# Norms of layer 2 beside the 7x7 attention of the next sample, images loaded ahead of the spectra, first transforms interleaved

## The chip, the core and the metric

The kernel runs on one core of a Trainium2 chip, in one launch. All data are float32. The time is the device time of one execution in microseconds (us); lower is better. A core has five engines with an instruction queue each: PE (matrix products, whose weight loads are listed as PEld), DVE and ACT (element-wise work), POOL (GpSimd) and SP, which here issues DMA transfers only. An engine executes its queue in order; between engines, semaphores order the work.

## The reference

Four layers are applied to an image batch `x` of shape (4, 56, 56, 128), each as `x = x + layer(groupnorm(x))`. Layer 0 is an attention over 7x7 windows followed by attention over all 3136 tokens and an MLP; layer 1 is an edge layer; layer 2 is a spectral attention; layer 3 a convolution. The change lies where layer 2 begins:

```python
xa = x.reshape(B * T, 1, H, W)                 # B=4 samples, T=128 channels, 56x56
xa_n = _inorm(xa, norm_g[0], norm_b[0])        # instance norm of each image
k = _fno_layer(xa_n, wK, wKs, bKs, (H // 2, W // 2))
q = _fno_layer(xa_n, wQ, wQs, bQs, (H // 2, W // 2))
v = _fno_layer(xa_n, wV, wVs, bVs, (H, W))
...
xf = jnp.fft.rfft2(x, norm='forward')          # inside _fno_layer, by _spec_conv
...
attention = _inorm(projd + xa, norm_g[1], norm_b[1])
```

Here `x` is already group-normed, in 32 groups of 4 channels, over the whole image. The kernel computes both norms of a sample from the same row statistics and does the Fourier transforms as matrix products.

## The kernel before

Channels lie on the 128 partitions, the 56x56 image of a sample (3136 values, 12.5 KB) along each partition.

**Samples one after the other.** `build` (from L2320 on) runs `first_layers` for b = 0 to 3. It loads `xw` (L2397, SP), calls `fast_attention`, which first calls `fast_windows` (attention in 7x7 windows) and then does the attention over all tokens, then `mlp` and `edge_layer`. These write the result in place into the one tile `x1`, and SP stores it to `x2d[b]` in DRAM (L2403). All of this stands in a branch that is taken when the scores are small; the other branch holds a general form that does not run on these inputs.

**The windows.** `fast_windows` handles the image in NG = 8 groups of 392 tokens (8 windows of 49). It is a software pipeline written out by hand: in iteration n of 19, group n is projected (`project`, L360 to L365), group n-1 scored (L379), n-2 multiplied with the values (`value`, L394 to L398), n-3 transposed (`turn`, L406), n-4 projected out (`output`, L416), and n-5 to n-11 go through a layer norm (`central` L421, `variance` L431 to L436, `divide` L443) and the projections of the next attention (`attended`, L451 to L462). In `variance`, every fourth group (HALF = 4), a root on ACT and a reciprocal on DVE are made for four groups at once (`w_r`, L434 and L435). Three PSUM banks, handed out in turn by `bank()`, take most products. PE, ACT and DVE run in the order in which the code stands (`manual_schedule`); only POOL and SP are left to the scheduler.

**The spectra.** After the fourth sample, `spectra` is the first stage of layer 2. For each sample, `normed_images` takes row statistics (56 `bn_stats` of 56 values, L1188), aggregates them (L1192), averages over the four channels of a group by products with small matrices (`s_pt`, L1194 and L1210), norms the image in place (`apply_norm`, L192, called at L1215), stores it to `xad` for later (L1216), and finds mean and deviation of each row of the instance norm (L1219 to L1233, two more `s_pt` products) into `st.norm`. `sample_spectra` then transforms along rows (112 pairs of products into `s_pr`, L1250, in four quarters, each scaled into tile `s_z` by DVE at L1252 and copied by ACT at L1254), and from `s_z` makes three sets of spectra: `s_ps` (L1260, copied to S and iS by ACT at L1263), `s_pr2` (L1272, listed as `s_pr`, copied to R at L1276) and `s_px` (32 products in eight banks, L1282, copied to `xh` by DVE and ACT in turn, L231 and L229). The fourth sample comes first, since its image is still in `x1`; the other three are loaded again from `x2d` into two tiles (L1182). Both functions are generators: the norm of the next sample is advanced by one step after each step of the present sample's spectra. `value_weights` and `all_score_weights` prepare weights on POOL at the same time. `attention_weights` follows the stage; it uses S, iS and R.

Of the kernel before, what the change touches and what calls it, by code (L numbers as in the profile page):

```python
# [11 lines left out]
F32 = mybir.dt.float32  # L12
# [6 lines left out]
P = 128  # L19
B = 4  # L20
HH = 56
# [277 lines left out]

def both_attentions(k, w, xw, xf):  # L300
    window_attention(k, w, xw, xf)
    global_attention(k, w, xf)


def fast_windows(k, w, xw, xf, mr, Q, K, V):

# [15 lines left out]
    with ExitStack() as es:  # L322
# [103 lines left out]
        def variance(g):  # L426
            q = g % HALF
            if q == 0:
                roots[g // HALF] = psum.tile([P, 512], F32, tag="var", name="w_var", bufs=1)
            var = roots[g // HALF]  # L430
            nc.tensor.matmul(var[32 * q:32 * q + 32, :N], k.ones_c[:, 0:32], squares.pop(g), start=True, stop=True)  # L431
            if q == HALF - 1:
                r = wk.tile([P, N], F32, name="w_r")
                nc.scalar.activation(r, var[:, :N], AF.Sqrt, scale=1024.0, bias=eps)  # L434
                nc.vector.reciprocal(r, r)  # L435
                roots[g // HALF] = r  # L436
# [9 lines left out]
        def attended(g):  # L446
# [7 lines left out]
            while chunk < 25 and (g == NG - 1 or chunk * P + 4 * P <= b.stop):  # L454
# [8 lines left out]
                chunk += m  # L463

        norm(0)
        norm(1)
        for n in range(NG + 11):
            for stage, g in ((norm, n + 2), (project, n), (score, n - 1), (value, n - 2), (turn, n - 3), (output, n - 4),
                             (central, n - 5), (variance, n - 6), (attended, n - 11), (divide, n - 10)):
                if 0 <= g < NG:  # L470
                    stage(g)


# [85 lines left out]

def fast_attention(k, w, xw, xf, mr):  # L560

# [8 lines left out]
    with ExitStack() as es:  # L570
# [3 lines left out]
        va = big.tile([P, 25, P], F32, name="f_va")  # L574
        fast_windows(k, w, xw, xf, mr, qT, kT, va)

# [589 lines left out]

def normed_images(k, w, st, b, pools, x2d, xad, ready):

    nc = k.nc
    wk, psum = pools

    def tiny(name):
        return wk.tile([P, HH], F32, name="s_" + name)

    if st.last == b:
        xp = st.x1
    else:
        xp = wk.tile([P, HH + 1, HH], F32, name="s_x2")  # L1180
        for t in range(0, HH, 28):
            nc.sync.dma_start(xp[:, t:t + 28, :], x2d[b, :, t:t + 28, :])  # L1182
        yield
    nc.vector.memset(xp[:, HH, :], 0.0)
    x = xp[:, :HH, :]
    rows = wk.tile([P, HH, 6], F32, name="s_rows")
    for t in range(HH):
        nc.vector.bn_stats(rows[:, t, :], x[:, t, :])  # L1188
        if t % 8 == 7:
            yield  # L1190
    mv = wk.tile([P, 2], F32, name="s_mv")
    nc.vector.bn_aggr(mv, rows.rearrange("p a b -> p (a b)"))  # L1192
    ps = psum.tile([P, 512], F32, tag="t", name="s_pt")
    nc.tensor.matmul(ps[:, 0:1], k.g4, mv[:, 0:1], start=True, stop=True)  # L1194

    half = [rows[:, :, i] for i in range(6)]
    mean, sq, d = tiny("mean"), tiny("sq"), tiny("d")
    nc.vector.tensor_sub(d, half[1], half[4])
    nc.vector.tensor_mul(d, d, d)
    nc.vector.tensor_add(sq, half[2], half[5])  # L1200
    nc.vector.scalar_tensor_tensor(sq, d, HH / 4, sq, ALU.mult, ALU.add)
    nc.vector.tensor_add(mean, half[1], half[4])
    yield
    mr = wk.tile([P, 2], F32, name="s_mr")
    t1 = wk.tile([P, 1], F32, name="s_t1")
    nc.vector.tensor_copy(mr[:, 0:1], ps[:, 0:1])
    nc.vector.tensor_sub(t1, mv[:, 0:1], mr[:, 0:1])
    nc.vector.tensor_mul(t1, t1, t1)
    nc.vector.tensor_add(t1, t1, mv[:, 1:2])
    nc.tensor.matmul(ps[:, 1:2], k.g4, t1, start=True, stop=True)  # L1210
    yield
    nc.scalar.activation(t1, ps[:, 1:2], AF.Sqrt, bias=k.eps)
    yield
    nc.vector.reciprocal(mr[:, 1:2], t1)
    apply_norm(k, x, x, mr)  # L1215
    nc.sync.dma_start(xad[b], x)  # L1216
    ready[b] = xp
    yield
    nc.vector.tensor_scalar(mean, mean, 0.5, mr[:, 0:1], ALU.mult, ALU.subtract)  # L1219
    nc.vector.tensor_scalar_mul(mean, mean, mr[:, 1:2])  # L1220
    nc.vector.tensor_scalar(sq, sq, mr[:, 1:2], mr[:, 1:2], ALU.mult, ALU.mult)
    nc.tensor.matmul(ps[:, 64:64 + HH], k.ones_c, mean, start=True, stop=True)
    yield
    nc.vector.tensor_copy(st.norm[:, b, 0, :], ps[:, 64:64 + HH])
    nc.vector.tensor_sub(d, mean, st.norm[:, b, 0, :])
    nc.vector.tensor_mul(d, d, d)
    nc.vector.scalar_tensor_tensor(sq, d, float(HH), sq, ALU.mult, ALU.add)
    nc.tensor.matmul(ps[:, 128:128 + HH], k.ones_px, sq, start=True, stop=True)
    yield
    nc.scalar.activation(d, ps[:, 128:128 + HH], AF.Sqrt, bias=k.eps)  # L1230
    yield
    nc.vector.reciprocal(d, d)
    nc.vector.tensor_scalar_mul(st.norm[:, b, 1, :], d, w.ng[:, 0:1])  # L1233
    yield


def sample_spectra(k, st, b, pools, x):

# [4 lines left out]

    z = wk.tile([P, 33, 2 * HH], F32, name="s_z")
    xf = x.rearrange("p t h -> p (t h)")
    for t0 in range(0, HH, 14):
        ps = psum.tile([P, 512], F32, tag="row", name="s_pr")
        for t in range(14):
            for ri in range(2):
                nc.tensor.matmul(ps[64 * ri:64 * ri + 64, t * 33:(t + 1) * 33],  # L1250
                                 xf[:, (t0 + t) * HH:(t0 + t) * HH + 64], k.fw[:, ri, :], start=True, stop=True)
        nc.vector.tensor_mul(z[:, :, t0:t0 + 14], ps[:, :462].rearrange("p (t f) -> p f t", t=14),  # L1252
                             bc(st.norm[:, b, 1, t0:t0 + 14], 1, 33))
        nc.scalar.copy(z[:, :, HH + t0:HH + t0 + 14], z[:, :, t0:t0 + 14])  # L1254
        yield
    o = slice(64 * (b % 2), 64 * (b % 2) + 64)
    for c0, c1, v in C_BLOCKS_S:
        ps = psum.tile([P, 512], F32, tag="acc", name="s_ps")
        m = (c1 - c0) * HH
# [8 lines left out]
    for blocks in (C_BLOCKS_R[:2], C_BLOCKS_R[2:]):  # L1268
        ps = psum.tile([P, 512], F32, tag="acc", name="s_pr2")
        for i, (c0, c1, v) in enumerate(blocks):  # L1270
# [8 lines left out]
    for c0 in range(0, 32, 4):  # L1279
        ps = psum.tile([P, 512], F32, tag="acc", name="s_px")  # L1280
        for i in range(4):
# [5 lines left out]

def spectra(k, w, st, x2d, xad):

# [3 lines left out]
    for t in (st.S, st.iS, st.R):  # L1293
        nc.gpsimd.memset(t[:, :, :, HH:], 0.0)
    ready = {}
    with ExitStack() as es:
# [4 lines left out]
                                                     mybir.EngineType.DVE}))  # L1301

        order = [st.last] + [b for b in range(B) if b != st.last]
        norms = [normed_images(k, w, st, b, (wk, tiny), x2d, xad, ready) for b in order] + [iter(())]
        next(norms[1])
        for _ in norms[0]:
            pass
        for n, b in enumerate(order):
            ahead = norms[n + 1]
            for _ in sample_spectra(k, st, b, (wk, psum), ready.pop(b)):  # L1310
                next(ahead, None)
            for _ in ahead:
                pass

# [1032 lines left out]
def build(k, packs, I, out):  # L2347
# [3 lines left out]
    with ExitStack() as es:  # L2351
# [10 lines left out]

        l2p = es.enter_context(tc.tile_pool(name="l2", bufs=1))
        with tc.tile_pool(name="w01", bufs=1) as wp, tc.tile_pool(name="io", bufs=1) as io:
            xw = io.tile([P, TOK], F32, name="xw")
# [29 lines left out]
            def first_layers(attention, x, to, loaded=False):  # L2395
# [6 lines left out]
                edge_layer(k, w1, x1, st)  # L2402
                nc.sync.dma_start(to, x1)  # L2403

            with tc.If(small_scores > 0) as small:
                for b in range(B):
                    first_layers(lambda *a: fast_attention(*a, k.mr[:, b, :]), I["x"][b], x2d[b],
                                 loaded=b == 0)
            with small.Else():
                with tc.For_i(0, B, 1) as b:  # L2410
                    first_layers(both_attentions, I["x"][bass.ds(b, 1)].rearrange("b p t -> (b p) t"),
                                 x2d[bass.ds(b, 1)].rearrange("b p l n -> (b p) l n"))

        l3p = es.enter_context(tc.tile_pool(name="l3", bufs=1))
        load_weights(k, l3p, I, "w3_", w2)
        load_weights(k, l3p, I, "w2_", w2, only=CONV_WEIGHTS)
        st = Env()
        st.x1, st.last = x1w, B - 1
        st.norm = l3p.tile([P, B, 2, HH], F32, name="norm")
        st.AbT = l3p.tile([P, 2, HH], F32, name="AbT")  # L2420
        st.dc = l3p.tile([1, B, HH], F32, name="dc")
        with tc.tile_pool(name="xh", bufs=1) as xp:
            st.xh = xp.tile([112, B, 2, 32, HH], F32, name="xh")
            with tc.tile_pool(name="sp", bufs=1) as sp:
# [4 lines left out]
                with tc.tile_pool(name="g_wk", bufs=1, side="right") as wk:  # L2429
                    all_score_weights(k, I, w2, sp, wk, st)  # L2430
                    value_weights(k, I, w2, wk, dd)
                    spectra(k, w2, st, x2d, xad)
                x1s.close()
# [32 lines left out]
```

## Time and profile before

| | |
|---|---|
| median of 5 runs | 3930.84 us (3921.26 to 3940.58) |
| the profiled execution | 3928.13 us, span 3926.3 us |
| mean granted PE clock | 0.955 |
| busy PE / DVE / ACT / POOL | 3551.4 / 2883.7 / 2050.1 / 1200.9 us (90 / 73 / 52 / 31%) |
| DMA | 111.12 MB, mean 28 GB/s |
| x2d stores of samples 0 to 3 issued | first at 762.2, last at 2896.6 us |
| spectra stage | from the last edge operation (DVE, 2895.83 + 0.68) to the last copy of xh (ACT, 3037.73 + 0.53) |

The profile gives, for each instruction, its line, engine, operation, output and inputs, its start and length, and how long its engine had been idle before it and on whom it had waited ("[3.47 <-DVE s_mv L1192]"). "Granted clock" is the share of the full PE clock that the chip allowed. The chain of waits is followed back from the last instruction to whatever released each one. A tile is shown without its number, so `s_x2` appears as `s_x`, `w_h1` as `w_h` and `x1` as `x`.

### The profile page before, as it was taken

The numbers are of one execution on the slowest core, as the hardware profiler recorded it, in microseconds if no ns is written. First come the engines' busy times: TensorE is split into PE (matmuls) and PEld (weight loads), VectorE is DVE, ScalarE is ACT, GpSimd is POOL, SyncE is SP. The second block draws the span as 40 slices with busy tenths as digits, with TensorE's granted clock in tenths as the row PEclk, the third lists the DMA queues.
The fourth block names the chain that finished last, engine by engine and source line by source line (L and its number), as shares of the span: only waits on it lengthen the run. The fifth ranks groups of instructions, "written<-read, shape, count | busy, mean of one in ns | idle before, by whom it ended". The sixth has DMA issues, their size and how long they took to land. (4 is left out here: it accounts for less than half of the span.)

```text
span 3926.3 us, 79380 instructions
## 1 busy us (share of the span) xinstructions
PE 3551.4 (90%) x35416; PEld 1589.5 (40%) x35416; DVE 2883.7 (73%) x2667; ACT 2050.1 (52%) x2056; POOL 1200.9 (31%) x671
## 2 busy tenths in 40 slices
PE   6899998989998899999889999998977989999988
PEld 4322234542223455222245532224446433336554
DVE  6588867758887685888768568885975767775764
ACT  4577755557775444777555467773532002215332
POOL 0000006600000560000037100001860769984665
PEclk9999999999999999999999999998978999999988
DMA  2000000000000000000000000000022048842101
GB/s 94 1 1 1 1 1 19 19 1 1 1 1 1 18 3 18 1 1 1 1 17 3 18 1 1 1 1 0 3 77 96 1 91 165 176 95 83 58 9 50
DMA packets 73496, 111.12 MB, mean 28 GB/s; under 512 B 62140, under 2 KB 63932, under 8 KB 67900
## 3 DMA queue, kind: packets, MB, share of 16 engines
q1 hardware_dynamic: 14460, 93.13, 8.0%
q10 hardware_dynamic: 58688, 12.85, 2.0%
q8 instruction: 279, 4.57, 0.5%
q14 instruction: 69, 0.57, 0.0%
HBM read 79.46 MB, written 26.51 MB: 27 GB/s over the span
## 5 line engine op out<-in xcount | busy, mean ns | idle before, releaser
L641 ACT ACTIVATE f_ring<-f_s 128x1792 f32<-128x1792 f32 (+3 forms) x796 | 1098.5, 1430 | 316.6 <-PE f_s L639 314.4
L594 DVE TENSOR_TENSOR f_acc<-f_acc,f_ring 128x1792 f32<-128x1792 f32 x560 | 1134.0, 2025 | 81.1 <-ACT f_ring L641 27.2
L639 PE MATMUL f_s<-f_qT,f_kT 32*128 32x448 f32 x5376 | 740.5, 573 | 57.9 <-ACT f_ring L641 33.7
L883 POOL TENSOR_TENSOR x<-xf,xw 128x343 f32<-128x343 f32 (+2 forms) x36 | 29.9, 832 | 2129.6 <-issue 2057.3
L600 PE MATMUL f_po<-f_ring,f_va 128*32 128x448 f32 x5376 | 592.0, 548 | 0.0
L967 DVE TENSOR_TENSOR e_td<-e_pa,e_c 128x1792 f32<-128x1792 f32 x252 | 491.4, 2014 | 8.0 <-ACT e_a L934 8.0
L969 POOL TENSOR_TENSOR e_tp<-e_a,e_c 128x1792 f32<-128x1792 f32 x140 | 451.7, 3259 | 144.5 <-PE e_acc L974 104.6
L639 PEld LDWEIGHTS f_s<-f_qT,f_kT 32*128 32x128 f32 x5376 | 268.5, 183 | 539.0 <-ACT f_ring L641 369.7
L974 PE MATMUL e_acc<-e_td,t_shared 32*32 32x448 f32 x8064 | 322.3, 545 | 23.6 <-DVE e_td L967 13.1
L971 ACT ACTIVATE e_tp<-e_tp 128x1792 f32<-128x1792 f32 x140 | 235.2, 1697 | 184.9 <-POOL e_tp L969 184.9
L1568 DVE TENSOR_TENSOR u_ud<-u_px,u_d 112x1792 f32<-112x1792 f32 x144 | 240.1, 1708 | 95.1 <-PE u_po L1573 86.0
L600 PEld LDWEIGHTS f_po<-f_ring,f_va 128*32 128x32 f32 x5376 | 133.0, 109 | 399.9 <-issue 398.9
L974 PE MATMUL e_acc<-e_tp,t_shared 32*32 32x448 f32 x4480 | 220.6, 544 | 2.5 <-ACT e_tp L971 2.2
L1573 PE MATMUL u_po<-u_ud,AT 112*64 112x448 f32 x960 | 200.7, 548 | 23.7 <-DVE u_ud L1568 23.7
L1570 POOL TENSOR_TENSOR u_up<-xh,u_d 112x1792 f32<-112x1792 f32 x64 | 193.7, 3056 | 24.1 <-PE u_po L1573 12.4
L974 PEld LDWEIGHTS e_acc<-e_td,t_shared 32*32 32x32 f32 x8064 | 133.6, 103 | 149.0 <-DVE e_td L967 59.0
L594 DVE TENSOR_TENSOR f_acc<-f_ring 128x1792 f32<-128x1792 f32 x28 | 56.7, 2024 | 106.5 <-ACT f_ring L641 77.5
L1573 PE MATMUL u_po<-u_up,AT 112*64 112x448 f32 x576 | 125.1, 541 | 0.9 <-POOL u_up L1570 0.9
L1573 PEld LDWEIGHTS u_po<-u_ud,AT 112*64 112x64 f32 x960 | 64.8, 137 | 148.0 <-issue 86.6
L974 PEld LDWEIGHTS e_acc<-e_tp,t_shared 32*32 32x32 f32 x4480 | 94.4, 103 | 54.7 <-ACT e_tp L971 18.5
L856 ACT ACTIVATE m_hT<-m_ph,w_fb 128x392 f32<-128x392 f32 x128 | 72.8, 589 | 73.0 <-PE m_ph L855 67.5
L612 DVE RECIPROCAL f_den<-f_s 128x448 f32<-128x448 f32 x28 | 82.8, 2956 | 37.6 <-PE f_s L610 37.6
(460 smaller groups left out, 4752.8 us busy)
## 6 DMA issues: line engine op xcount, KB each, us to landing
u_d<-dd SPq DMA_DIRECT2D x48, 784.0 KB
xw<-in_x SPq DMA_DIRECT2D x4, 1568.0 KB
x2d<-x SPq DMA_DIRECT2D x4, 1568.0 KB
x_xs<-xad ACTq DMA_DIRECT2D x32, 196.0 KB
xm<-x_ev ACTq DMA_DIRECT2D x64, 98.0 KB
o_a<-xm SPq DMA_DIRECT2D x8, 784.0 KB
o_x<-x2d SPq DMA_DIRECT2D x4, 1568.0 KB
out<-o_o SPq DMA_DIRECT2D x12, 448.0 KB
```

What stands on the lines that cost most here:

```text
L594: nc.vector.tensor_add(acc, slots(j, 0) if c == 1 else acc, slots(j, c))
L600: nc.tensor.matmul(po[heads[h], :NB], va[o, c, heads[h]], p, start=(c == 0), stop=(c == 24))
L612: nc.vector.reciprocal(den, pd[:, 0, :NB])
L639: nc.tensor.matmul(ss[:, i, :NB], kT[heads[h], c * P:(c + 1) * P], qT[heads[h], blk(j)], start=True, stop=True)
L641: nc.scalar.activation(ring[:, slot:slot + m, :], ss[:, :m, :NB], AF.Exp, scale=scale)
L967: nc.vector.tensor_tensor(t, am, cm, ALU.max)
L969: nc.gpsimd.tensor_sub(t, bc(a.rearrange("p (l n) -> p l n", l=8), 1, 4), cm)
L971: nc.scalar.activation(tf, tf, AF.Relu)
L974: nc.tensor.matmul(acc[quarters[q], r, :NB], k.ident[o, o], t[o, q].rearrange("p l n -> p (l n)"), start=(g == 0), stop=(g == len(EDGE_TUR ...
L1568: nc.vector.tensor_mul(u, bc(px[:, :, :NB], 2, m), dm)
L1570: nc.gpsimd.tensor_mul(u, bc(x, 2, m), dm)
L1573: nc.tensor.matmul(po[64 * b2:64 * b2 + 64, :NB], st.AT[:, 8 * i + h0 + q, 2 * bp + b2, :], u[:, b2, q, :], start=(left == 16), stop=(left ...
```

## The change

**The norms move.** `normed_images` is now started by `first_layers` and handed to `fast_windows` as `beside`. While sample b goes through its windows (b = 1, 2, 3), the image of sample b-1, still in `x1`, is normed in place. One step follows each iteration n, except in n = 9 and 13, where the step (a root on ACT) stands inside `variance`, behind the root of `w_r`. The steps: 14 `bn_stats` in each of n = 0 to 3; aggregate, first product, five small operations and a copy in n = 4; three small ones in n = 5; second product and ACT's copy in n = 6; root in n = 9; reciprocal, `apply_norm`, store to `xad` and three small ones in n = 10; third product and four operations in n = 11; fourth product and copy in n = 12; root in n = 13; reciprocal and a scaling in n = 14. The products take banks of the windows' own `bank()`. The roots now read a copy in SBUF instead of PSUM. The norm of sample 3 stays in `spectra`, beside the spectra of samples 0 and 1.

**Images.** The normed images of samples 0, 1 and 2 are loaded from `xad`, not from `x2d`, into two tiles of a new pool `x2` on the right-hand side of SBUF. The loads of 0 and 1 are issued right after the branch, ahead of all weight loads. The store of sample 3 to `x2d` is issued after them. `st.norm` is allocated earlier, and the zero row below an image is written by POOL instead of DVE.

**Transforms.** `sample_spectra` is split. `first_transform` holds the row transform. `spectra` does the transform of sample 0 whole; then, within the spectra of sample b, the four quarters of the transform of b+1 stand after steps 2, 5, 7 and 9 of 13. The order of samples is 0, 1, 2, 3. The pool of PSUM tag "acc" has four banks instead of three.

The branch that does not run gets the same norms in a loop of its own after its samples; it is left out below.

```diff
@@ fast_windows
             if q == HALF - 1:
                 r = wk.tile([P, N], F32, name="w_r")
                 nc.scalar.activation(r, var[:, :N], AF.Sqrt, scale=1024.0, bias=eps)
+                next(steps, None)
                 nc.vector.reciprocal(r, r)
...
+        steps = beside(bank)
         norm(0)
         norm(1)
         for n in range(NG + 11):
...
                 if 0 <= g < NG:
                     stage(g)
+            if n not in (HALF + 5, 2 * HALF + 5):
+                next(steps, None)
+        for _ in steps:
+            pass
@@ normed_images
-def normed_images(k, w, st, b, pools, x2d, xad, ready):
+def normed_images(k, w, st, b, wk, bank, xp, xad):
...
-    if st.last == b:
-        xp = st.x1
-    else:
-        xp = wk.tile([P, HH + 1, HH], F32, name="s_x2")
-        for t in range(0, HH, 28):
-            nc.sync.dma_start(xp[:, t:t + 28, :], x2d[b, :, t:t + 28, :])
-        yield
-    nc.vector.memset(xp[:, HH, :], 0.0)
...
         nc.vector.bn_stats(rows[:, t, :], x[:, t, :])
-        if t % 8 == 7:
+        if t % 14 == 13:
             yield
...
-    ps = psum.tile([P, 512], F32, tag="t", name="s_pt")
+    ps = bank()
     nc.tensor.matmul(ps[:, 0:1], k.g4, mv[:, 0:1], start=True, stop=True)
...
+    nc.vector.tensor_copy(mr[:, 0:1], ps[:, 0:1])
     yield
...
     nc.vector.tensor_add(t1, t1, mv[:, 1:2])
+    yield
+    ps = bank()
     nc.tensor.matmul(ps[:, 1:2], k.g4, t1, start=True, stop=True)
-    yield
-    nc.scalar.activation(t1, ps[:, 1:2], AF.Sqrt, bias=k.eps)
+    var = wk.tile([P, 1], F32, name="s_var", bufs=1)
+    nc.scalar.copy(var, ps[:, 1:2])
+    for _ in range(3):
+        yield
+    nc.scalar.activation(t1, var, AF.Sqrt, bias=k.eps)
     yield
     nc.vector.reciprocal(mr[:, 1:2], t1)
     apply_norm(k, x, x, mr)
-    nc.sync.dma_start(xad[b], x)
-    ready[b] = xp
-    yield
+    nc.sync.dma_start(xad, x)
...
+    yield
+    ps = bank()
     nc.tensor.matmul(ps[:, 64:64 + HH], k.ones_c, mean, start=True, stop=True)
-    yield
...
+    yield
+    ps = bank()
     nc.tensor.matmul(ps[:, 128:128 + HH], k.ones_px, sq, start=True, stop=True)
+    nc.scalar.copy(d, ps[:, 128:128 + HH])
     yield
-    nc.scalar.activation(d, ps[:, 128:128 + HH], AF.Sqrt, bias=k.eps)
+    nc.scalar.activation(d, d, AF.Sqrt, bias=k.eps)
@@ spectra
-        for _ in norms[0]:
+        norm = normed_images(k, w, st, B - 1, wk, lambda: tiny.tile([P, 512], F32, name="s_pt"), st.x1, xad[B - 1])
+        zs = {}
+        first = [first_transform(k, st, b, (wk, psum), st.x1 if b == B - 1 else images(b), zs) for b in range(B)]
+        for _ in first[0]:
             pass
-        for n, b in enumerate(order):
-            ahead = norms[n + 1]
-            for _ in sample_spectra(k, st, b, (wk, psum), ready.pop(b)):
-                next(ahead, None)
-            for _ in ahead:
-                pass
+        for b in range(B):
+            for n, _ in enumerate(sample_spectra(k, st, b, (wk, psum), zs.pop(b))):
+                next(norm, None)
+                if b < B - 1 and n in (2, 5, 7, 9):
+                    next(first[b + 1])
@@ build
-                nc.sync.dma_start(to, x1)
+                if to is not None:
+                    nc.sync.dma_start(to, x1)
+
+            def norms(b, bank):
+                if b < 0:
+                    return iter(())
+                return normed_images(k, w2, st, b, io, bank, x1w, xad[b])
...
                 for b in range(B):
-                    first_layers(lambda *a: fast_attention(*a, k.mr[:, b, :]), I["x"][b], x2d[b],
-                                 loaded=b == 0)
+                    first_layers(lambda *a: fast_attention(*a, functools.partial(norms, b - 1), k.mr[:, b, :]), I["x"][b],
+                                 x2d[b] if b < B - 1 else None, loaded=b == 0)
...
+        x2p = x2s.enter_context(tc.tile_pool(name="x2", bufs=2, side="right"))
+
+        def images(b):
+            if b not in loaded:
+                xp = loaded[b] = x2p.tile([P, HH + 1, HH], F32, name="s_x2")
+                for t in range(0, HH, 28):
+                    nc.sync.dma_start(xp[:, t:t + 28, :], xad[b, :, t:t + 28, :])
+                nc.gpsimd.memset(xp[:, HH, :], 0.0)
+            return loaded[b]
+
+        loaded = {}
+        for b in range(2):
+            images(b)
+        nc.sync.dma_start(x2d[B - 1], x1)
```

## The prediction

> **What bounds the kernel now.** I looked first at the chain of waits between 2880 and 3050 us, because the change empties this stretch, the spectra stage. Its columns are start, length and what ran.
>
> ```profile
> 2898.86 6.71 DVE s_rows L1188 x56
> ...
> 2917.68 12.12 PE s_pr L1250 x224
> ...
> 2998.19 1.68 DVE s_mv L1192
> 2999.91 0.48 PE s_pt L1194 x2
> ...
> 3019.46 7.19 PE s_pr L1250 x224
> 3027.46 1.23 PE s_ps L1260 x4
> ...
> 3031.93 5.77 PE s_px L1282 x56
> ```
>
> The chain hops between DVE (norms) and PE (transforms), so the stage is bound by neither alone. The same stage as a timeline of PE, with the idle time before each group in brackets:
>
> ```profile
> 2999.91 0.48 PE L1194 MATMUL s_pt<-s_mv,t_shared 128*128 128x1 f32 x2 [3.47 <-DVE s_mv L1192]
> ...
> 3010.38 0.65 PE L1222 MATMUL s_pt<-s_mean,c_ones_c 128*128 128x56 f32 x2 [2.49 <-DVE s_mean L1220]
> ...
> 3027.46 1.87 PE L1260 MATMUL s_ps<-s_z,t_images 128*128 128x56 f32 x6 [0.84 <-DVE s_z L1252]
> 3029.26 1.07 PE L1272 MATMUL s_pr<-s_z,t_images 128*64 128x448 f32 x6
> 3030.84 6.85 PE L1282 MATMUL s_px<-t_images,s_z 128*112 128x112 f32 x64 [0.51 <-ACT iS L1263]
> ```
>
> PE stands while DVE makes the next sample's norm, four times a sample. The last sample, with no norm beside it, takes 1.87 + 1.07 + 6.85 us. Third, busy time by stretch (length; PE, PEld, DVE, ACT, POOL busy; granted PE clock; DMA):
>
> ```profile
> 2980.00:2985.00 5.00, 4.47 (x23) 4.47 (x24) 1.11 (x4) 0.74 (x2) 0.00 (x0) 0.50 0.30 125
> ...
> 3020.00:3025.00 5.00, 5.00 (x170) 5.00 (x167) 1.28 (x2) 1.19 (x3) 0.00 (x0) 0.95 0.01 3
> ...
> 761.00:861.00 100.00, 88.83 (x729) 54.94 (x728) 53.88 (x102) 47.74 (x80) 8.77 (x22) 0.97 0.04 17
> 2896.50:3038.30 141.80, 94.95 (x1232) 83.81 (x1232) 82.98 (x362) 34.29 (x77) 36.07 (x57) 0.74 0.32 115
> ```
>
> The stage lasts 141.8 us with a clock of 0.74: the waits also cost clock (0.50 in 2980 to 2985, where the 64 matmul records of s_px go at half pace). The 7x7 windows of sample 1 (761 to 861), where three norms go, have DVE busy 54 of 100 us but PE 89 of 100. So half of DVE is free there, but its gaps are waits inside a chain with PE. The timeline, DVE then PE:
>
> ```profile
> 776.29 0.62 DVE L224 TENSOR_SCALAR w_qd<-w_mm,t_first 32x392 f32<-32x392 f32 x1 [2.14 <-ACT w_qd L222]
> ...
> 782.56 0.21 DVE L397 RECIPROCAL w_rec<-w_po 128x8 f32<-128x8 f32 x1 [0.66 <-PE w_po L394]
> ...
> 829.29 0.57 DVE L424 COPY w_h<-w_mm 128x392 f32<-128x392 f32 x1 [2.92 <-ACT w_sq L423]
> ```
> ```profile
> 820.00 0.82 PE L416 MATMUL w_mm<-w_oT,t_first 128*128 128x392 f32 x2
> ...
> 824.85 0.92 PE L443 MATMUL w_mm<-w_r,c_ones 32*128 32x392 f32 x2 [2.42 <-ACT w_oT L229]
> 825.71 1.65 PE L416 MATMUL w_mm<-w_oT,t_first 128*128 128x392 f32 x2
> ```
>
> From 776 to 824 PE shows no wait; any DVE delay there that reaches PE is lost for good. And after 2.42 us of idling, the same matmul took 1.65 us in place of 0.82.
>
> **The spectra stage, gain.** It ends at 3038.3, with ACT's last copy of xh. In the changed kernel it starts with the first transform of sample 0, whose image is already normed. DVE's last edge operation ends at 2896.5 and its next starts at 2898.9 (2.35 us of issue after the branch); I take 2898.9 for PE too. A transform at full clock took 6.73 us (the one at 2954.14), so 2905.6; 0.84 to s_ps: 2906.4.
> - Sample 0. PE does s_ps 1.87, the first quarter of the next transform 1.7 and s_pr2 1.07, to 2911.1. Then s_pt stands ahead of s_px in PE's order and needs s_mv. DVE by then has 42 statistics (6.71/56 = 0.12 us each, 5.0 us), one s_z 0.64, 14 more (1.7) and the aggregate 1.67: 2915.3. PE idles some 4.2 us. Left for PE: s_px 6.85, three quarters of a transform 5.1, four norm products about 2.0 (0.38, 0.59, 0.40, 0.68), some 14 us; the second product waits another 0.5 for DVE, which also prepares layer-3 weights. For the half clock after the idle I add 3 us (the bounds are 0, and 12 where s_px and transform all go at half pace). 2915.3 + 14 + 0.5 + 3: end 2932.8.
> - Samples 1 and 2: 1.87 + 1.07 + 6.85 + 6.9 = 16.7 us each, no norm beside them except the last two steps. ACT has 8.1 us of copies in each, DVE 5, so PE is the bound. The fourth PSUM bank of "acc" keeps s_px off ACT's copies. End 2966.2.
> - Sample 3: 10.8 us, as from 3027.46 to 3038.3. End 2977.0.
>
> Gain 61.3 us; 69 without the clock and s_mv losses, 50 with a late image (a rival below). POOL's weight preparation started on a load that landed at 2903.9 and handed its last result to SP at 2944.9; it still starts on a load behind the same last edge sample, ends before 2977, and what then follows on every engine is unchanged.
>
> **The queues.** SP's loads of images 0 and 1 come after the branch. Their tile lies where 25 KB of attention tiles lay, by the sizes in the code clear of the edge layer's tiles, so they can land around 2600, hidden under 300 us of edge layer. Sample 3's x2d store and the weight loads stand behind them and still go at about 2897. Image 2's load stands behind twelve weight loads (SP issued them by 2908 before) and is needed at about 2935. x2d plus weights plus image, 5.6 MB by my count of the sizes, at the 292 GB/s of 2897 to 2918 take 19 us: hidden. The xad stores inside the windows stand ahead of the next xw load, which waits for POOL some 480 us later: nothing. xad of sample 3 stands behind POOL's dd store (2945) and is read only at 3188: nothing. On POOL the pad memset of image 2 waits for the transform of image 0 (2905.6); behind it stands work that waited for t_w_qkr until 2911 anyway: nothing. If the landing of image 2 lost its cover it would cost its lateness in sample 1.
>
> **The windows, price.** Per sample DVE gets 56 statistics (6.7), the aggregate with five small operations and a copy (2.8, from the row at 2966.32 to 2968.9), three small ones (0.6), reciprocal, apply_norm and three (2.8, from 2975.01), four (1.0) and two (0.7): 14.6 us. PE gets the four products, 2.05. I replay sample 1 by the order in which the instructions now stand.
> - n=0: 14 statistics (1.68) against an idle of 0.48: shift 1.2. n=1: the gaps of 0.75 and 2.14 (ACT's 1.28 us table load) take them; the shift stays. n=2: no gap, 2.9. n=3: the gap of 0.66 is used, 3.9.
> - n=4: gaps 0.78 and 0.20 are used, 2.8 added: 5.7. Here the wait is PE's too: the s_mv product stands in PE's order ahead of projection 5, so all of PE stands from about 792.2 until the aggregate at 794.6, 2.4 us.
> - n=5 to 9: PE is full, so the 5.7 stay, and three small DVE operations hide. n=10: 2.8 us in the gap of 2.92 at 829.29. n=11: 1.0 in a gap of 2.26. n=14: 0.7 in 2.6. ACT's two copies and two roots (0.3 each) fall into gaps; the roots follow w_r's, so no further table load of 1.28.
> - Three of the four products fall where PE is full: 1.3. The 2.4 us idle at n=4 is the size of the row at 824.85, after which L416 and L421 took 1.65 and 1.51 for 0.82: 1.5 lost.
>
> Sum 8.5 us a sample, 25.5 for three. Bounds: 6 (the products alone, DVE covered) and 50 (14.6 + 2.05, all exposed). I take 25.5, as PE has hardly a gap to give back before 824.
>
> The Trainium skill (TensorE: Matmul & The Clock Gate, "What's actually happening") has the clock fall to half only after an idle window of about 3.4 us. The row at 824.85 shows it halved after 2.42 us, so the measurement decides. By the rule the 1.5 us at n=4 would drop out, and the sum would be 4.5 us better. The same section's 3.4 us of sustained work before the clock returns is what could speak against the change; rival C prices that from rows.
>
> **Sum.** -61.3 + 25.5 = -35.8 on the profiled execution's 3928.1 us (span 3926.3 and 1.8 around it), which is 2.7 under the median of the runs, 3930.8: 3892.3 there, 3895 for the median.
>
> **The rivals.**
> A. The windows hide nearly all. For it: DVE is 54% busy there. Against it: the gaps are chain waits of 0.5 to 0.8 us, shorter than 1.68. Price 7 instead of 25.5: 3877.
> B. Nothing hides: price 50, so 3920. Against it: the 2.14, 2.92 and 2.63 us gaps.
> C. Slower. The small stalls of n=0 to 4 leave PE's clock at half as in 2980 to 2985, through the full stretch 789 to 822: 33 us of matmuls become 66. With the 7 that is 40 a sample, 120 in all: 3990. It decides from about 13 us of such work a sample (61.3/3 = 20.4, less the 7.0 of shift and products). Against it: 780 to 820 holds clock 1.00 although 774 to 780 had waits.
> D. The change does not do what it says at the start: the images wait for the edge layer's last tiles, go out at 2897, and 3.2 MB at 292 GB/s give 11 us. Gain 50: 3906.
>
> **How the numbers follow.** Forecast 0.50, A 0.20, D 0.12, B 0.10, C 0.08. Own range of the forecast 3882 to 3908. The range goes from 3869 (a gain of 69, a price of 7) to 3917 (B, with 2 to 3 us of its products hidden), leaving out C and part of B. A measurement of this kernel can tell 0.3%, 11.8 us: faster is below 3919.0. All of A, D and the forecast and half of B are faster, 0.87; the other half 0.05; C slower 0.08.
>
> **What would show it.** Right: the spectra some 80 us long, clock above 0.9 from sample 1 on, PE idle about 4 us before the first s_pt there; each of the windows 1 to 3 some 7 to 10 us longer than 99, with a wait of PE for s_mv near its 30th us; s_x loads issued before 2700. Wrong: windows clock below 0.9 (C), s_x issued after 2896 (D), waits for s_pt growing past the stage, or POOL ending after 2977.

## The result, and the profile after

The changed kernel takes 3929.6 us (median of 42 runs, 3914.7 to 3951.6), the kernel before 3930.9 (79 runs, 3921.1 to 3944.4). The ratio is 0.9999 with a 95% interval of 0.9993 to 1.0005: no difference that can be told, where 36 us had been forecast.

Both kernels were profiled again, before five times in all and after three times, because one execution differs from the next by several microseconds. The span cut at three events that both kernels have (us, mean of the profiles, extremes in brackets):

| stretch | before (5) | after (3) | difference |
|---|---|---|---|
| start to the first x2d store (sample 0, no norm beside it) | 761.1 (757.4 to 762.2) | 765.2 (761.3 to 769.1) | +4.1 |
| from there to the end of the edge layer of sample 3 (three windows with a norm) | 2133.6 (2128.2 to 2135.6) | 2162.3 (2158.1 to 2164.9) | +28.7 |
| the spectra, to the last copy of xh | 141.1 (140.3 to 141.8) | 106.4 (105.6 to 107.7) | -34.7 |
| from there to the end | 888.2 (886.5 to 891.1) | 895.7 (894.2 to 896.8) | +7.5 |

So the windows cost about what the forecast said (25.5), and the spectra gave 35 us where it said 61. The three windows with a norm took 106.8 to 108.5 us each, counted from the end of the edge layer to the first score product of the attention behind them; before they took 97.9 to 99.7. The other two rows are stretches in which the change alters nothing; they come back with runs r1 to r7.

Where the spectra lost their gain, in the table of busy times by stretch of the changed kernel (stretch, length, busy PE, PEld, DVE, ACT, POOL, granted PE clock, DMA share, GB/s). The stretches are the first transform, samples 0, 1 and 2, sample 3, and all together:

```profile
2927.19:2942.69 15.50, 11.99 (x225) 11.63 (x225) 2.62 (x6) 1.76 (x4) 2.73 (x13) 0.62 0.81 241
2942.69:2989.61 46.92, 27.19 (x308) 23.39 (x309) 37.69 (x101) 8.72 (x20) 31.59 (x45) 0.62 0.20 76
2989.61:3022.80 33.19, 33.19 (x602) 29.37 (x602) 10.83 (x18) 15.52 (x36) 0.00 (x0) 1.00 0.08 29
3022.80:3032.75 9.95, 9.38 (x78) 7.73 (x76) 2.54 (x5) 6.32 (x14) 0.42 (x1) 1.00 0.16 42
2927.19:3032.75 105.56, 81.75 (x1208) 72.12 (x1208) 53.67 (x127) 32.32 (x72) 34.74 (x58) 0.77 0.25 82
```

Samples 1 to 3 run as forecast, PE without a gap at full clock: 33.2 us for two and 9.95. Sample 0 takes 46.9 us in place of 26.4, the first transform 15.5 in place of 9.9. In sample 0 DVE is busy for 37.7 us and POOL for 31.6. The chain of waits of the changed kernel (start, length, what ran; "issue" is time in which an engine waited for nothing that the profile shows), where before had its hops between norm and transform:

```profile
2927.79 2.39 issue
2930.18 6.58 PE s_pr L1255 x127
2936.94 5.03 PE s_pr L1255 x46
...
2952.17 1.58 DVE s_mv L1190
2953.75 3.93 DVE s_d L1196
2957.78 9.73 DVE t_w_M L1685
...
2974.70 0.59 PE s_pt L1210 x2
```

It runs through DVE: a subtraction of 56 elements for 3.93 us and a scaling of 62 for 9.73. Neither is a matter of work. The profile of before has the same two:

```profile
2907.48 0.19 DVE L1198 TENSOR_TENSOR s_d<-s_rows 128x56 f32<-128x56 f32 x1
...
2907.66 0.19 DVE L1676 TENSOR_SCALAR t_w_M<-t_w_M 112x62 f32<-112x62 f32 x1
```

Timelines of the changed kernel there, DVE first, then POOL, then PE:

```profile
2949.37 1.74 DVE L1186 BATCH_NORM_STATS2 s_rows<-x 128x6 f32<-128x56 f32 x14
...
2953.67 4.01 DVE L1196 TENSOR_TENSOR s_d<-s_rows 128x56 f32<-128x56 f32 x1
...
2957.78 9.73 DVE L1685 TENSOR_SCALAR t_w_M<-t_w_M 112x62 f32<-112x62 f32 x1
2965.35 2.17 DVE L1197 TENSOR_TENSOR s_d<-s_d 128x56 f32<-128x56 f32 x1
...
2968.88 0.24 DVE L1200 TENSOR_TENSOR s_mean<-s_rows 128x56 f32<-128x56 f32 x1
...
2969.56 0.18 DVE L1685 TENSOR_SCALAR t_w_M<-t_w_M 112x62 f32<-112x62 f32 x1
```
```profile
2942.02 0.14 POOL L2449 MEMSET s_x<- 128x56 f32 x1 [10.36 <-PE s_pr L1255]
...
2953.77 1.25 POOL L1378 TENSOR_TENSOR q_g<-q_g,q_t 128x512 f32<-128x512 f32 x1
2954.99 0.24 POOL L1368 TENSOR_TENSOR t_w_qk<-t_w_qk,q_skip 128x32 f32<-128x32 f32 x1
2955.20 1.13 POOL L1339 TENSOR_TENSOR d_d<-t_w_P,d_m 128x448 f32<-128x448 f32 x1
2956.30 1.26 POOL L1377 TENSOR_TENSOR q_t<-t_w_qk 128x512 f32<-128x512 f32 x1
...
2968.97 1.45 POOL L1348 TENSOR_SCALAR d_t<-t_w_V,t_images 128x448 f32<-128x448 f32 x1
```
```profile
2953.80 0.59 PE L1192 MATMUL s_pt<-s_mv,t_shared 128*128 128x1 f32 x2 [4.16 <-DVE s_mv L1190]
...
2974.70 0.59 PE L1210 MATMUL s_pt<-s_t,t_shared 128*128 128x1 f32 x2 [13.73 <-DVE s_t L1207]
```

POOL's weight arithmetic for the scores and values runs back to back from 2942.0 to 2974.4, just beside sample 0's part of the norm. DVE's element-wise operations from SBUF to SBUF (SBUF is the memory that holds the tiles, PSUM the one that takes the products) stand meanwhile, that is, they last many times their usual length; bn_stats (14 in 1.74 us, as ever) does not. They stand beside POOL's TENSOR_TENSOR operations, which have two inputs; beside its TENSOR_SCALAR at 2968.97 the same kinds took 0.24 and 0.18 us. PE waits 13.73 us for s_t behind them.

In before POOL worked at the same hour, from 14.5 us after the edge layer (14.8 here), but it idled until 2911 for t_w_qkr while DVE passed that place (2905.8 to 2910.7). Here POOL's next operation, the pad of image 2, waits 10.36 us for the first transform, and the whole run starts behind it. Where DVE and POOL did meet in before, some operations stood as well (DVE, then POOL):

```profile
2914.53 1.27 DVE L1226 TENSOR_TENSOR s_d<-s_d 128x56 f32<-128x56 f32 x1
...
2936.58 2.95 DVE L1201 SCALAR_TENSOR_TENSOR s_sq<-s_d,s_sq 128x56 f32<-128x56 f32 x1
```
```profile
2911.02 1.84 POOL L1353 TENSOR_TENSOR t_w_qk<-t_w_qk,t_w_qkr 128x32 f32<-128x32 f32 x1 [4.94 <-DMA t_w_qkr<-in_w_qkr]
```

The rest went as drawn: the image loads were issued at 2708.2, under the edge layer, and the windows show the wait that was forecast for their n=4 (PE of the changed kernel, sample 1):

```profile
801.47 0.56 PE L1192 MATMUL w_mm<-s_mv,t_shared 128*128 128x1 f32 x2 [2.39 <-DVE s_d L1196]
801.88 1.65 PE L361 MATMUL w_mm<-w_xg,t_first 128*128 128x392 f32 x2
```

### The profile page after: what moved, and what is told of

It is laid out like the page before. It is cut to its first block, busy times and chain, and to the rows that moved or that the text cites. A ratio compares the mean times of both kernels' runs of the same rounds, so it can differ in the third digit from the quotient of the medians.

```text
span 3928.8 us, 79379 instructions
## 1 busy us (share of the span) xinstructions
PE 3564.2 (91%) x35416; PEld 1593.6 (41%) x35416; DVE 2894.6 (74%) x2663; ACT 2048.7 (52%) x2064; POOL 1199.6 (31%) x675
## 5 line engine op out<-in xcount | busy, mean ns | idle before, releaser
L981 PE MATMUL e_acc<-e_td,t_shared 32*32 32x448 f32 x8064 | 323.1, 545 | 25.6 <-DVE e_td L974 14.9
L1579 POOL TENSOR_TENSOR u_up<-xh,u_d 112x1792 f32<-112x1792 f32 x64 | 193.8, 3054 | 26.4 <-PE u_po L1582 13.0
L1444 POOL TENSOR_TENSOR q_u<-iS,q_g 128x1792 f32<-128x1792 f32 x32 | 102.8, 3237 | 75.6 <-PE s_px L1293 52.5
```

Of the source, the lines that this page charges most:

```text
L981: nc.tensor.matmul(acc[quarters[q], r, :NB], k.ident[o, o], t[o, q].rearrange("p l n -> p (l n)"), start=(g == 0), stop=(g == len(EDGE_TUR ...
L1579: nc.gpsimd.tensor_mul(u, bc(x, 2, m), dm)
```

## The experiments

All start from the changed kernel. Times are medians; ratios are to runs of the kernel before on the same chip, whose medians were 3928.5 in the first group of four and 3926.4 in the second. After's own ratio is to the 3930.9 above. Stretches come from one profile each, cut as in the table above; the profiled execution can lie some way from the median (e7_spread_late's by 16 us, e2_norm_late's by 12).

| | time | ratio to before, 95% | first transform | samples 0, 1, 2, 3 | spectra | store to edge end |
|---|---|---|---|---|---|---|
| after | 3929.6 | 0.9999 (0.9993 to 1.0005) | 15.5 | 46.9, 16.6, 16.6, 10.0 | 105.6 | 2158.1 |
| e1_conv_late | 3928.2 | 1.0002 (0.9991 to 1.0013) | 15.6 | 38.3, 16.6, 16.6, 9.9 | 97.0 | 2163.6 |
| e2_norm_late | 3929.7 | 1.0005 (0.9992 to 1.0018) | 16.9 | 32.3, 27.9, 18.1, 9.9 | 105.0 | 2161.4 |
| e4_no_pool | 3919.7 | 0.9977 (0.9967 to 0.9987) | 21.2 | 28.3, 18.2, 16.6, 9.9 | 94.2 | 2163.6 |
| e5_both_late | 3917.5 | 0.9978 (0.9969 to 0.9988) | 16.1 | 21.0, 32.0, 16.6, 9.9 | 95.6 | 2163.6 |
| e3_no_window_norms | 3900.2 | 0.9937 (0.9919 to 0.9955) | 14.2 | 47.8, 21.1, 16.6, 9.9 | 109.6 | 2134.6 |
| e6_spread | 3909.1 | 0.9958 (0.9943 to 0.9972) | 14.9 | 18.4, 21.0, 17.8, 9.9 | 82.0 | 2159.7 |
| e7_spread_late | 3893.7 | 0.9914 (0.9898 to 0.9930) | 14.8 | 18.2, 22.6, 17.7, 9.9 | 83.3 | 2143.0 |
| e8_serial | 3929.4 | 1.0003 (0.9986 to 1.0020) | 15.4 | 45.4, 17.0, 16.9, 10.0 | 104.6 | 2163.8 |

**e1_conv_late: DVE's weight preparation out of sample 0.**

```diff
-        load_weights(k, l3p, I, "w3_", w2)
-        load_weights(k, l3p, I, "w2_", w2, only=CONV_WEIGHTS)
...
                     spectra(k, w2, st, xad, images)
+                    load_weights(k, l3p, I, "w3_", w2)
+                    load_weights(k, l3p, I, "w2_", w2, only=CONV_WEIGHTS)
```

> The loads of the layer-3 and convolution weights come after the spectra, so DVE's preparation of them leaves sample 0; POOL's weight arithmetic and the norm of sample 3 stay beside each other there. Theory T1 (the 20.5 us that sample 0 took over the forecast are DVE's small operations kept waiting while POOL computes; both DVE's own norm operations and the weight preparation pay): about half of the stretched operations are gone, sample 0 takes some 36 us in place of 46.9, time about 3919. Rival T2 (the weight preparation was only pulled along, the norm's own chain is what waits): sample 0 stays within 3 us of 46.9, time 3928 to 3931. Rival T3 (the delay is PE's halved clock after the branch and not DVE): no change, and the waits of PE for s_mv and s_t stay at 4 and 13 us.

Sample 0 took 38.3 us, 8.6 less. The norm's own operations still stand beside POOL (DVE, then PE):

```profile
2955.34 4.02 DVE L1197 TENSOR_TENSOR s_d<-s_d 128x56 f32<-128x56 f32 x1
...
2959.69 2.56 DVE L1199 SCALAR_TENSOR_TENSOR s_sq<-s_d,s_sq 128x56 f32<-128x56 f32 x1
```
```profile
2967.18 0.58 PE L1210 MATMUL s_pt<-s_t,t_shared 128*128 128x1 f32 x2 [4.77 <-DVE s_t L1207]
```

PE's wait fell from 13.73 to 4.77. T1 holds in the profile (36 expected), T2 and T3 do not. The time did not show it: 3919 was expected, and the interval reaches down only to 0.9991. Where the 8.6 us went is not shown.

**e2_norm_late: the norm of sample 3 from sample 1 on, weight preparation left in sample 0.**

```diff
-                next(norm, None)
+                next(norm, None) if b > 0 else None
```

> The norm of sample 3 starts with sample 1 of the spectra in place of sample 0; the weight preparation stays in sample 0, where DVE then stands between POOL's operations with it. T1: PE no longer waits for s_t in sample 0, but its s_z and xh copies stand behind the weight preparation on DVE, so sample 0 takes 24 to 32 us, sample 1 17 to 22 (POOL ends in its course), sample 2 17; the stage is some 90 us in place of 105.6, time about 3914. T3: sample 0 still above 40 us, time 3926 to 3931.

Sample 0 came to 32.3 us, just above the 24 to 32 of T1, and far below the 40 of T3. The wait moved to a later product (PE):

```profile
2967.87 4.81 PE L1293 MATMUL s_px<-t_images,s_z 128*112 128x112 f32 x24 [11.01 <-ACT xh L230]
```

Its PSUM bank is freed by an ACT copy of xh, which stood behind ACT's copy of an s_z, which waited 17.97 us for DVE, where that s_z was queued behind the preparation (two operations of 4.11 and 7.70 us among them). Sample 1 was a miss: 27.9 us against 17 to 22, and so the stage and the time. Either of the two DVE jobs alone, beside POOL, stops PE; and a norm beside sample 1 costs more than its work. e5 takes that up.

**e4_no_pool: POOL's arithmetic left out.** The score and value weights are constants here, so the output is another.

```diff
-    score_weights(nc, wk, w.qk, w.qkr, w.qks, k.qm, st.g)
...
+    nc.gpsimd.memset(st.g, 0.01)
+    nc.gpsimd.memset(st.g4, 0.01)
...
+    nc.gpsimd.memset(f, 0.01)
```

> Leaves out POOL's arithmetic on the score and value weights (their results are set to 0.01), everything else as in the changed kernel. T1: DVE's small operations fall back to 0.15 to 0.35 us, PE waits for s_t under 1 us in place of 13.7, sample 0 takes 26 to 30 us, time about 3911. T3 (halved clock, or DVE's own amount of work): sample 0 stays above 40 us, time 3927 to 3931.

```profile
2937.18 11.84 PE L1255 MATMUL s_pr<-t_images,s_x 128*64 128x33 f32 x218 [5.45 <-issue]
...
2959.50 0.38 PE L1192 MATMUL s_pt<-s_mv,t_shared 128*128 128x1 f32 x2 [3.23 <-DVE s_mv L1190]
...
2965.42 0.45 PE L1210 MATMUL s_pt<-s_t,t_shared 128*128 128x1 f32 x2
```

And sample 0 by engine (columns as above):

```profile
2949.75:2978.07 28.32, 23.24 (x309) 19.83 (x309) 19.25 (x101) 8.71 (x20) 0.00 (x0) 0.80 0.24 88
```

Sample 0 took 28.3 us, as T1 said and within 2 of the forecast's 26.4, and the wait for s_t is gone. T3 falls. Of the 18.6 us by which it is shorter than in the changed kernel, 14.7 are time in which PE stood (19.7 there, 5.1 here); in the other 4.0 the changed kernel's PE works on the same products at a lower clock (0.62 against 0.80). The spectra as a whole gained only 11.4, since the first transform here paused twice (3.32 and 5.45 us of "issue") where after paused once for 2.39, and took 21.2 us; with so long a first transform, part of the 4.0 may be the clock's and not POOL's.

**e5_both_late: both edits, so that only s_z and copies of xh lie beside POOL.** The diffs are those of e1 and e2.

> Both: the norm of sample 3 starts with sample 1 and the loads of the layer-3 and convolution weights come after the spectra, so that beside POOL's run DVE has only s_z and the xh copies. T1: sample 0 takes 18 to 21 us, sample 1 17 to 22, samples 2 and 3 17 and 10; the stage is 80 to 86 us with the slow first transform of 15.5, time about 3907, faster than both kernels. Rival T2b (s_z and the copies of xh are kept waiting by POOL just as the small operations are): sample 0 30 us or more, time 3917 to 3925.

Sample 0 took 21.0 us: s_z and the copies read PSUM and lasted 0.64 and 0.62 us beside a busy POOL, so T2b falls. But sample 1 took 32.0, though DVE's operations were now short. Its PE timeline, and the clock by stretch (columns as above):

```profile
2975.07 0.59 PE L1192 MATMUL s_pt<-s_mv,t_shared 128*128 128x1 f32 x2 [4.51 <-DVE s_mv L1190]
2975.52 1.81 PE L1293 MATMUL s_px<-t_images,s_z 128*112 128x112 f32 x8
2977.26 3.20 PE L1255 MATMUL s_pr<-t_images,s_x 128*64 128x33 f32 x56
```
```profile
2975.10:2981.00 5.90, 5.90 (x69) 5.64 (x70) 3.72 (x11) 0.00 (x0) 1.88 (x3) 0.50 0.44 146
2981.00:2986.00 5.00, 5.00 (x53) 4.80 (x54) 1.73 (x7) 1.17 (x3) 0.00 (x0) 0.50 0.17 28
2986.00:2991.00 5.00, 5.00 (x51) 4.74 (x50) 1.49 (x7) 1.30 (x3) 0.00 (x0) 0.50 0.01 2
```

After one wait of 4.51 us PE ran 15.9 us without a gap at a granted clock of 0.50; the same quarter of a transform takes 3.20 there and 1.82 at full clock. So a wait of 4.5 us costs some 8 more. The kernel is nonetheless 0.2% faster than before and than the changed kernel.

**e3_no_window_norms: the norms of samples 0 to 2 left out**, images stored unnormed.

```diff
-                if b < 0:
-                    return iter(())
+                return iter(())
```

> Leaves out the norms of samples 0 to 2 beside the windows: the images are stored unnormed, and their factors are set to 1. All else is the changed kernel. Theory W1 (the forecast's price of 25.5 us holds): time 3904, the three windows after the first shorter by 8.5 us each. Rival W2 (the price is 28 to 30, as the stretch from the first x2d store to the end of the edge layer reads in four of the five profiles of changed kernels, 27.1 to 29.3 over before): 3900 to 3902. Rival W3 (most of it is hidden): above 3918.

The stretch from the first store to the end of the edge layer came back to 2134.6, before's value. The price is what the changed kernel has over that: 23.5, 30.3 and 29.3 us in its three profiles. The times differ by 24.4 (0.9937 against 0.9999 of 3930.9), with some 7 either way. W3 falls; W1 and W2 are not told apart, and need not be.

**e8_serial: the interleaving undone.**

```diff
-                if b < B - 1 and n in (2, 5, 7, 9):
-                    next(first[b + 1])
+            for _ in first[b + 1] if b < B - 1 else ():
+                pass
```

> The changed kernel with the interleaving undone: the first transform of a sample follows the whole of the sample before. I1 (samples 1 and 2 are bound by PE alone, 16.6 us in either order): within 3 us a sample, time 3928 to 3936. Rival I2 (the interleaving hides copies and s_z, which PE would otherwise wait for): 4 us or more a sample, time 3940 or more.

I1: 0.3 us a sample. The interleaving is worth nothing that shows. That samples 1 to 3 are short goes with their having no norm beside them: with one, sample 1 took 27.9 us (e2) and 32.0 (e5).

**e6_spread: the norm in ten steps.** As e5, with the aggregate a step ahead of its product, and the statistics beside sample 0, where bn_stats does not mind POOL:

```diff
+        if t in (18, 37, 55):
+            yield
...
     nc.vector.bn_aggr(mv, rows.rearrange("p a b -> p (a b)"))
+    yield
...
+SPREAD = ((0, 4), (0, 7), (0, 10), (1, 3), (1, 6), (1, 7), (1, 9), (1, 11), (2, 0), (2, 1))
...
-                next(norm, None) if b > 0 else None
+                next(norm, None) if (b, n) in SPREAD else None
```

> As e5_both_late, but the norm of sample 3 is cut into ten steps with the aggregate one step ahead of its product: 56 statistics beside sample 0, the rest beside sample 1 and the start of sample 2. Theory C1 (in e5 the 15.3 us that sample 1 takes over the 16.7 of an undisturbed one are one wait of 4.5 us for s_mv, and a granted clock that stays at half for some 15 us after it; both go when PE never waits over 2 us): sample 1 takes 18 to 20 us in place of 32.0, the stage 82 to 85 in place of 95.6, time about 3906. Rival C2 (the norm's work itself, on DVE and PE, takes the time): sample 1 stays above 27 us, time 3914 to 3918.

```profile
2962.00 0.29 PE L1258 MATMUL s_pt<-s_mv,t_shared 128*128 128x1 f32 x2
...
2965.21 0.38 PE L1274 MATMUL s_pt<-s_t,t_shared 128*128 128x1 f32 x2 [2.03 <-DVE s_t L1271]
```

The wait for s_mv is gone, the one for s_t is 2.03 us with POOL still at work. The stage takes 82.0 us in place of 95.6 with the same work in it, and sample 1 21.0 in place of 32.0, one more than C1 allowed. C1 holds in the main, C2 falls. Two things changed at once, the aggregate's place and that of the statistics, which here lie beside sample 0, so the gain isn't shared out between them.

**e7_spread_late: the same ten steps in the windows, from n=10 on.**

```diff
-                next(steps, None)
                 nc.vector.reciprocal(r, r)
...
-            if n not in (HALF + 5, 2 * HALF + 5):
+            if n >= 10:
```

> As e6_spread, and the norms beside the windows use the same ten steps from n=10 on, where DVE has gaps of 2 to 2.9 us in each step. W4 (the price of the windows is the place and not the work: shifts at n=0 to 4 where PE is full, and the wait for s_mv with its half clock): the windows cost 1 to 2 us a sample in place of 8.5 to 9.8, time 20 to 25 below e6_spread, about 3884. Rival W5 (it is the work: PE or DVE late anyway, or the last steps run past the end of the windows): less than 10 below e6_spread.

```profile
826.54 2.33 DVE L1250 BATCH_NORM_STATS2 s_rows<-x 128x6 f32<-128x56 f32 x19
828.79 0.55 DVE L425 COPY w_h<-w_mm 128x392 f32<-128x392 f32 x1
832.41 0.56 DVE L445 TENSOR_TENSOR w_h<-w_h,w_mm 128x392 f32<-128x392 f32 x1 [3.06 <-PE w_mm L444]
...
838.06 2.22 DVE L1250 BATCH_NORM_STATS2 s_rows<-x 128x6 f32<-128x56 f32 x18
840.19 2.59 DVE L436 RECIPROCAL w_r<-w_r 128x392 f32<-128x392 f32 x1
```
```profile
843.93 1.64 PE L452 MATMUL w_mm<-w_h,w_fq 128*128 128x392 f32 x2 [2.36 <-DVE w_h L445]
```

The first 19 statistics fill a gap of DVE and delay nothing; the last 18 stand ahead of the second reciprocal of w_r, and PE waits 2.36 us and runs on at half clock. The price fell to 8.4 us for the three (2143.0 against 2134.6; 9.1 in a second profile), about 3 a sample: most of W4's claim, though the cutting into ten steps and the later start were changed together. The time is 15.4 below e6_spread, between what W4 and W5 said. At 0.9914 of before this is the best version found.

**r1 to r6, the kernels once more, and r7_spread_late_again.** No new edit. Four expectations, the others being the same:

> The kernel before, profiled once more. N1 (what the first two profiles show ahead of the first x2d store, 762.2 against 769.1 us, and behind the spectra, 888.0 against 896.1, belongs to the execution and not to the change): the stretch behind the spectra lies anywhere from 887 to 900 us, the first store anywhere from 761 to 769. Rival N2 (the change costs 8 us behind the spectra and up to 7 in sample 0): 888 within 2, and 762 within 2.

> The changed kernel, profiled once more. N1: the stretch behind the spectra anywhere from 887 to 900 us, the first store from 761 to 769. N2: 896 within 2 and 769 within 2. Sample 0 of the spectra within 3 us of 46.9 by both; the stretch from the first x2d store to the end of the edge layer 24 to 30 us over the 2134.3 of before by both.

> The kernel before, profiled a third time. N1 (the stretch behind the spectra differs by the execution): among three more profiles of before at least one has 894 us or more there. N2 (the change sets it): all of them within 2 of 888.

> e7_spread_late, profiled once more: its first profile lay 16 us under the median of its runs. N1: the stretch behind the spectra takes 894 to 900 us this time or the clock phases elsewhere account for it; its windows (8.7 us over before) and its spectra (83.3 us) repeat within 3.

Behind the spectra before took 888.0, 887.7, 887.8, 891.1 and 886.5 us; the changed kernel 896.1, 896.8 and 894.2. By these alone it would be the change. But the experiments, whose instructions there are the same, took 887.2 (e2), 888.7 (e8), 890.6 (e3), 888.0 and 887.4 (e7 and r7), and 895.0 to 900.2 (e1, e4, e5, e6). Neither N1 nor N2 holds as put. What differs is how long PE takes over the same matmuls (us, extremes of the profiles):

| stretch | matmuls | PE busy, before | PE busy, after | the rest, before | the rest, after |
|---|---|---|---|---|---|
| up to the first x2d store | 7286 | 674.6 to 681.3 | 679.3 to 687.8 | 80.9 to 82.8 | 80.9 to 82.0 |
| behind the spectra | 5376 | 793.4 to 797.3 | 802.3 to 806.0 | 93.2 to 93.9 | 90.8 to 91.9 |

The granted clock goes with it, but in phases: in three stretches of 20 us, one after the other from 700 us behind the spectra on, it was 0.59, 0.73 and 0.87 in after, and 0.83, 1.00 and 0.66 in e2_norm_late. Why one execution falls into the one pattern and another into the other stays open.

The changed kernel's sample 0 came again as 47.1 and 48.3 us, as r2 said, and its stretch with the windows 30.6 and 29.6 us above 2134.3, at the upper end of the 24 to 30. r7 repeated e7's windows, but behind the spectra it did not take the 894 to 900 that N1 said; its spectra took 87.3 us, 4.0 more, and its first store came at 768.9 in place of 761.6. These two make the 11 us by which it was slower than e7's first profile.

## Why the prediction was wrong

The forecast was 3895 in a range of 3869 to 3917; 3929.6 lies 35 us off and outside. By its steps:

- **Windows, +25.5: right, and somewhat low.** 28.7 by the means of the profiles (9.6 a sample for 8.5), 24 by the times of e3. The replay of waits from n=0 to n=4 named the place, the 2.4 us wait (2.39) and the half clock after it (1.65 for 0.82). Rivals A, B and C fall.
- **Images loaded first: right.** Issued at 2708.2; rival D falls.
- **Samples 1 to 3: right.** 16.6, 16.6 and 10.0 us against 16.7, 16.7 and 10.8.
- **First transform, "took 6.73 us (the one at 2954.14)": the wrong row.** 5.6 us more. The chain of waits that the prediction itself shows has the row for a PE that starts after a pause: 12.12 us for the same 224 matmuls at 2917.68. After a pause of 2.39 us it took 12 us here too; the clock returned only in sample 0.
- **Sample 0, "end 2932.8": the step that failed**, 46.9 us against 26.4. The sum had PE stand for 4.7 us (4.2 for s_mv, 0.5 for s_t) and work for 21.6 with its 3 us for half clock; it stood for 19.7, of which 4.16 for s_mv, as forecast, and 13.73 for s_t, and worked for 27.2. e4 takes POOL's work away and gets 28.3, so the sum without POOL was 2 short and POOL's company costs 18.6. Without the layer-3 preparation on DVE 8.6 of them go (e1, 38.3), without the norm 14.6 (e2, 32.3); the two share one queue, and their parts do not add up. The term that failed is the wait for s_t "for DVE, which also prepares layer-3 weights": 0.5 us forecast, 13.73 measured. The prediction did follow POOL, and asked when it would start and end and what waits behind it; it judged "behind it stands work that waited for t_w_qkr until 2911 anyway: nothing" and was right that POOL is not late. It did not ask what POOL's run lies beside. The profile of before held the hint in the rows above: 2.95 us for a 56-element operation at 2936.58, 1.27 at 2914.53, both while POOL worked, and 0.2 elsewhere; and on POOL's side 1.84 us in place of 0.25 at 2911.02, beside DVE's apply_norm (2910.84, 1.91 us).
- **Half clock after the wait, 3 us with bounds of 0 and 12: too low.** In e5, where PE met no second wait of that size, one wait of 4.5 us brought 15.9 us at half clock, about 8 us lost.
- **Interleaving** had no term of its own, and has none (e8).

The Trainium skill (SBUF — State Buffer, "SBUF: two separate sides") says that DVE and GpSimd share a pair of SBUF ports as an exclusive lock, which a DVE operation in a two-port mode or with two SBUF inputs takes, and that the loser blocks for the whole instruction. The rows agree in which kinds of DVE operation stand beside POOL's TENSOR_TENSOR and which do not; that they pass beside its TENSOR_SCALAR (2968.97) is not on the page. By "the whole instruction" the wait would be at most one POOL operation, up to 1.4 us here. Some waits were of that size (s_t at 2973.42 took 1.03 us), but the trace also has 4.01 and 9.73 us. POOL began 15 operations in the latter, so the loser does not always get its turn after one, nor in every TENSOR_SCALAR: the 9.73 us outlasted one of 1.39 at 2964.75. That the port is the cause is argued from these rows; shown is that POOL's company is.

The whole miss of 34.6 us: the spectra gave 26.6 less than forecast (34.7 for 61.3; in the first profile the first transform is 5.6 of this and sample 0 20.5), and the windows cost 3.2 more. That makes -6.0, and the medians of all runs differ by -1.2. The first and the last row of the table have the sign that would close this gap of 4.8, but with +4.1 and +7.5 more than its size: the profiled executions are not the median ones. Both rows are time in which PE took longer over the same matmuls; nothing was done to one of these stretches on purpose, so what slowed them is not shown.

## What to carry to other kernels

Work moved off one engine's wait must be laid beside what every other engine does at its new hour: look for a run of back-to-back POOL operations, and put beside it what the trace shows to be immune (bn_stats, reads of PSUM, as long as nothing that stands is queued ahead of them as in e2), not element-wise work from SBUF to SBUF. Here the long waits lay beside runs of POOL's two-input operations. A product that needs a reduction of DVE goes a step behind it in PE's order, since a wait of 2 to 5 us is paid again as half clock: e6, which also moved the statistics ahead, gained 13.6 us over e5's spectra with the same work. And where an engine is half idle, place the work in gaps as long as its pieces: the norm of the windows cost 24 to 30 us when begun at n=0 and 8 to 9 when begun at n=10 in ten steps.

## What was not expected of the hardware

- A DVE operation of 0.19 us took 9.73 (9.74 and 9.73 in the other two profiles) while POOL ran operations of 0.24 to 1.4 us without a break. Beside POOL's TENSOR_SCALAR of 1.45 us the same operation on the next matrix took 0.18.
- The granted clock returned slowly. In e5 PE stood for 4.51 us, then worked without a gap for 15.9 us at 0.50; in e1 the first transform and what follows had 0.50 for 21.1 us (2931.8 to 2952.9), with PE busy 20.3 of them. The Trainium skill (TensorE: Matmul & The Clock Gate, "What's actually happening") has full rate after some 3.4 us of sustained work; these rows do not agree.
- After the branch PE started six matmuls and then paused for 1.1 to 3.2 us, in e4 for 3.3 ahead of the six and 5.5 behind them, for which the profile names no releaser.
